# Exponentials row by row on ScalarE for three late score groups of a cross-attention kernel

## The chip, the core and the metric

The kernel runs on one core of one Trainium2 chip. The metric is device time in microseconds (us) of that core; before the change it is 498.44 us, the median of two runs (498.39 and 498.49). The engines are named as in the profile: PE is TensorE (matmuls), PEld its weight loads, DVE is VectorE, ACT is ScalarE, POOL is GpSimd, SP issues most DMAs.

## What is computed

The reference is an image-to-text cross-attention layer with two sets of keys, everything in float32:

```python
# x: (2, 2048, 640), ctx: (2, 154, 1024); 20 heads of 32
q = heads(x @ Wq.T)
text, ip = ctx[:, :77], ctx[:, 77:]
out  = softmax(q @ heads(text @ Wk.T).T / sqrt(32)) @ heads(text @ Wv.T)
out += softmax(q @ heads(ip @ Wk_ip.T).T / sqrt(32)) @ heads(ip @ Wv_ip.T)
return merge(out) @ Wo.T + bo + x
```

So each token and head has two softmaxes over 77 scores each. "A row" below is one such softmax: 77 neighbouring numbers in each of the 128 partitions (tokens).

## The kernel before

Channels lie on the partitions in chunks of 128, which is 4 heads. The work is cut into 20 units u: two images, 5 chunks of channels each, 2 halves of the tokens (1024) each. A unit's 8 tiles of 128 tokens form three groups s: groups 0 and 1 have 3 tiles, group 2 has 2 tiles. With 4 heads and 2 softmaxes per tile, a group of 3 tiles holds 24 rows and a group of 2 tiles holds 16.

The order of all work is written out by hand, in one long list of words (`SCHEDULE`). Each engine then works through its own instructions strictly in that order, and waits where an operand isn't ready or a buffer isn't free. The words for group s of unit u are, in the order in which one group needs them:

- `Rs.u@abcd`: the scores by PE, into four PSUM banks, one for each head (the digits; in the listings bank 0 is bank_79 and bank 7 is bank_86, so bank 1 is bank_80, bank 4 is bank_83, bank 5 is bank_84)
- `Ks.u`: ACT copies the four banks into `pb` in SBUF (line 238)
- `Ms.u`: DVE takes the maximum of each row (line 251)
- `Ss.u`: POOL, sometimes DVE, subtracts the maxima from the scores in place (line 265)
- `Es.u`: ACT takes the exponential, the whole group in one instruction (line 272)
- `Ds.u`, `Is.u`: DVE sums each row (line 297) and inverts the sums (line 304)
- `Ns.u`: POOL multiplies (line 309); `Ts.u`: DVE transposes in place (line 316)

`A.q` then multiplies two units' probabilities with the values on PE (line 325) into four banks, and `CA.q` copies these out on ACT (lines 348 and 352). Between these stand `q.u.h` (PE, a block of queries into one bank, line 194) and `cq.u.h` (ACT scales it into SBUF, line 204), and the products of the output projection: for the first image `m`, `cm`, `o` and `co` with their sums `G`; `p.i@b` (PE, line 464) is the last output chunk of the second image for token block i into bank b. After `A.9`, the last attention, the rest of the second image's projection follows (`F` and `Y`, lines 854 and 802, fed by weight and token sums `V` and `X` on DVE and POOL, lines 834 and 840).

The kernel already has code that takes a group's exponentials row by row, with the negated maximum as the instruction's bias (lines 274 to 284). It is used for a group whose `S` word is missing from the list; every group has one in this kernel.

Of the kernel before, what the change touches and what calls it, by code (L numbers as in the profile page):

```python
# [9 lines left out]
F32 = mybir.dt.float32  # L10
# [5 lines left out]
H, D, TEXT = 20, 32, 77  # L16
# [4 lines left out]
def kernel(  # L21
# [26 lines left out]
    P = 128  # L48
    NC = C // P
    NCC = CC // P  # L50
    G = P // D
# [19 lines left out]
    small = ctx.enter_context(tc.tile_pool(name="small", bufs=4))  # L71
# [141 lines left out]
    def keys_of(u, s):  # L213
        return pb_of(u, s)[:, :, :, : 2 * L]

    def rows_of(u, s):
        return keys_of(u, s).rearrange("p n g (t l) -> p (n g) t l", l=L)
# [26 lines left out]
    def rows_in(ps, n):  # L244
        return ps[:, : n * 2 * L].rearrange("p (n t l) -> p n t l", n=n, t=2)

    def maxima(u, s, ps=None):
        n = GROUPS[s][1] * G
        mx = small.tile([P, n, 2], F32, tag=f"mx{n}", name=f"mx_{u}_{s}")
        if ps is None:  # L250
            nc.vector.tensor_reduce(mx, rows_of(u, s), AX.X, ALU.max, negate=by_rows(u, s))  # L251
        else:
            for g in range(G):
                nc.vector.tensor_reduce(
                    mx.rearrange("p (n g) t -> p g n t", g=G)[:, g],
                    rows_in(ps[g], n // G),
                    AX.X,
                    ALU.max,
                    negate=True,
                )  # L260
        maxs[(u, s)] = mx
# [7 lines left out]
    def exponential(u, s, ps):  # L269
        if not by_rows(u, s):  # L270
            e = keys_of(u, s).rearrange("p n g l -> p (n g) l")
            nc.scalar.activation(e, e, AF.Exp)  # L272
            return
        n = GROUPS[s][1]
        for g in range(G):
            for t in range(n):
                for x in range(2):
                    row = rows_of(u, s)[:, t * G + g, x]
                    nc.scalar.activation(
                        row,  # L280
                        row if copied(u, s) else rows_in(ps[g], n)[:, t, x],
                        AF.Exp,
                        bias=maxs[(u, s)][:, t * G + g, x : x + 1],
                    )

    def copied(u, s):
        return f"K{s}.{u}" in planned

    def by_rows(u, s):
        return f"S{s}.{u}" not in planned  # L290

    dens = {}

# [257 lines left out]
    for t in range(2):  # L551
# [80 lines left out]
    planned = {w.partition("@")[0].removesuffix(".d") for w in SCHEDULE}  # L632
# [6 lines left out]
    def emit(word):  # L639
# [34 lines left out]
        elif k[0] in "KMSEDINT":  # L674
            ps = at[f"R{i}.{x}"]
            if k[0] == "K":
                take(x, i, ps)
            elif k[0] == "M":
                maxima(x, i, None if copied(x, i) else ps)
            elif k[0] == "E":  # L680
                exponential(x, i, ps)
            else:
                more = (eng,) if k[0] in "SN" else ()
                dict(S=subtract, D=sums, I=invert, N=normalise, T=transpose)[k[0]](x, i, *more)
# [94 lines left out]
    for c, stages in enumerate(chains_of):  # L779
        for _, text in stages:  # L780
            for _, t in terms(text):
                for h in range(NH):
                    o = int(t[0]), NH * int(t[1]) + h
# [113 lines left out]
```

## Time and profile before

| | |
|---|---|
| Timed runs | 498.39 and 498.49 us, median 498.44 |
| Span of the profiled execution, first to last instruction | 496.5 us |
| Outside the span (median less span; the profiled execution has no time of its own listed) | 1.9 us |
| PE busy | 489.3 us (99% of the span) |
| DVE busy | 441.2 us (89%) |
| POOL busy | 403.7 us (81%) |
| ACT busy | 241.9 us (49%) |
| Granted TensorE clock, mean | 0.999 |

In the profile's rows a time is counted from the start of the span. PE shows two records for each matmul. "x16" behind a row is the number of instructions merged into it, and the bracket names how long the engine had been idle before it and what released it. A released engine continues in its own order; idle time of an engine that nobody waits for costs nothing.

### The profile page before, as it was taken

What the parts mean: (1) busy time and instruction counts of PE and PEld (TensorE: products, weight loads), DVE (VectorE), ACT (ScalarE), POOL (GpSimd) and SP (SyncE); (2) the same over time, 40 slices, a digit from 0 to 9 for tenths busy, and PEclk for the clock granted to TensorE, in tenths of its full rate; (3) what the DMA queues carried; (4) which work ended last, traced back from release to release, by engine and by line L of the source; (5) the groups of instructions that cost most, each with busy time, mean ns of one, the idle gap of its engine ahead of it and who ended that gap; (6) DMA issues with size and microseconds to landing.
All of it is one profiled execution on the core that took longest, in us unless ns stands there. A gap on an engine that the chain in (4) does not pass through costs nothing.

```text
span 496.5 us, 9743 instructions
## 1 busy us (share of the span) xinstructions
PE 489.3 (99%) x4114; PEld 288.0 (58%) x4114; DVE 441.2 (89%) x404; ACT 241.9 (49%) x423; POOL 403.7 (81%) x173
## 2 busy tenths in 40 slices
PE   8999999999999999999999999999999999999996
PEld 4658548648647556456655655744766575444442
DVE  0078999999989989998999998899899999999886
ACT  1277557757747567567506635545764443100000
POOL 0079959999989999997995899799599999378770
PEclk9999999999999999999999999999999999999999
DMA  8980542511843735715577078345515012510026
GB/s 291 354 213 20 153 107 71 176 51 36 209 133 89 244 108 172 219 16 164 222 243 237 22 241 309 97 150 185 189 65 160 3 45 64 170 62 24 0 106 232
DMA packets 66956, 70.15 MB, mean 141 GB/s; under 512 B 3680, under 2 KB 46688, under 8 KB 66912
## 3 DMA queue, kind: packets, MB, share of 16 engines
q1 hardware_dynamic: 65648, 67.96, 44.0%
q10 hardware_dynamic: 1264, 1.57, 0.9%
q8 instruction: 32, 0.52, 0.4%
q14 instruction: 12, 0.10, 0.1%
HBM read 58.21 MB, written 11.30 MB: 140 GB/s over the span
## 4 chain that ended last, share of the span: by engine, by line
PE 91%; DVE 6%; DMA 1%; ACT 1%; ACTq 0%; issue 0%; DVEq 0%
PE bank L194 35%; PE bank L854 11%; PE bank L325 11%; PE bank L226 10%; PE bank L133 9%; PE bank L483 9%; PE bank L464 4%; PE bank L493 2%; DVE pb L316 2%; DMA x<-in_x_dram 1%; DVE den L297 1%; DVE mx L251 1%; DVE acc L508 0%; DVE acc L512 0%; ACT pb L238 0%
## 5 line engine op out<-in xcount | busy, mean ns | idle before, releaser
L309 POOL TENSOR_TENSOR pb<-pb,rden 128x1848 f32<-128x1848 f32 (+1 forms) x59 | 172.1, 2938 | 24.0 <-DVE rden L304 21.2
L265 POOL TENSOR_TENSOR pb<-pb,mx 128x1848 f32<-128x1848 f32 (+1 forms) x55 | 162.8, 2977 | 35.4 <-DVE mx L251 35.2
L194 PE MATMUL bank<-x,wq 128*128 128x512 f32 x400 | 178.6, 598 | 0.9 <-DMA wq<-in_L_xattn_Wq_dram 0.6
L251 DVE TENSOR_REDUCE mx<-pb 128x24 f32<-128x1848 f32 (+1 forms) x60 | 109.3, 1841 | 31.5 <-ACT pb L238 31.3
L194 PEld LDWEIGHTS bank<-x,wq 128*128 128x128 f32 x400 | 74.0, 190 | 89.3 <-issue 82.0
L238 ACT COPY pb<-bank 128x462 f32<-128x462 f32 (+1 forms) x240 | 102.0, 537 | 44.5 <-PE bank L226 43.9
L272 ACT ACTIVATE pb<-pb 128x1848 f32<-128x1848 f32 (+1 forms) x60 | 94.3, 1584 | 55.0 <-POOL pb L265 54.2
L297 DVE TENSOR_REDUCE den<-pb 128x24 f32<-128x1848 f32 (+1 forms) x60 | 110.0, 1840 | 5.9 <-ACT pb L272 5.7
L316 DVE STREAM_TRANSPOSE pb<-pb 128x1920 f32<-128x1920 f32 (+1 forms) x60 | 113.9, 1923 | 0.9 <-POOL pb L309 0.9
L226 PEld LDWEIGHTS bank<-kT,qT 32*128 32x128 f32 x1280 | 45.9, 184 | 23.6 <-issue 14.2
L226 PE MATMUL bank<-kT,qT 32*128 32x154 f32 x1280 | 56.5, 305 | 1.0 <-ACT pb L238 0.7
L325 PE MATMUL bank<-pb,v 32*32 32x512 f32 x1600 | 55.2, 597 | 0.1
L204 ACT ACTIVATE qT<-bank 128x512 f32<-128x512 f32 x40 | 23.6, 597 | 50.3 <-PE bank L194 50.3
L133 PE MATMUL bank<-wo_ct,aT 128*128 128x154 f32 x320 | 45.5, 296 | 0.0
L133 PEld LDWEIGHTS bank<-wo_ct,aT 128*128 128x128 f32 x320 | 43.0, 188 | 3.6 <-issue 2.7
L325 PEld LDWEIGHTS bank<-pb,v 32*32 32x32 f32 x1600 | 29.5, 103 | 22.9 <-issue 11.7
L464 PE MATMUL bank<-aT,wo_ct 128*128 128x512 f32 x80 | 36.3, 596 | 0.0
L483 PE MATMUL bank<-aT,wo_ct 128*128 128x256 f32 x128 | 32.8, 389 | 0.0
L802 DVE TENSOR_TENSOR x<-x,bank 128x512 f32<-128x512 f32 x36 | 23.6, 684 | 5.2 <-PE bank L854 4.6
L483 PEld LDWEIGHTS bank<-aT,wo_ct 128*128 128x128 f32 x128 | 23.3, 190 | 6.4 <-issue 3.7
L464 PEld LDWEIGHTS bank<-aT,wo_ct 128*128 128x128 f32 x80 | 15.0, 190 | 17.3 <-issue 17.1
L854 PE MATMUL bank<-pb 128*128 128x512 f32 x48 | 22.1, 593 | 0.0
(74 smaller groups left out, 347.6 us busy)
## 6 DMA issues: line engine op xcount, KB each, us to landing
x<-in_x_dram SPq DMA_DIRECT2D x20, 1280.0 KB, 7.7
out_dram<-acc SPq DMA_DIRECT2D x20, 256.0 KB, 2.6
acc<-in_x_dram SPq DMA_DIRECT2D x16, 256.0 KB, 4.0
x<-in_x_dram SPq DMA_DIRECT2D x15, 256.0 KB, 5.7
out_dram<-x SPq DMA_DIRECT2D x15, 256.0 KB, 2.0
v<-scr SPq DMA_DIRECT2D x40, 80.0 KB, 4.1
wq<-in_L_xattn_Wq_dram SPq DMA_DIRECT2D x9, 320.0 KB, 5.3
aT<-in_L_xattn_Wk_dram SPq DMA_DIRECT2D x5, 512.0 KB, 6.9
```

The source lines that it names most:

```text
L133: nc.tensor.matmul(keys_in(out), loaded[n][:, k, :], cT[:, k, :, t, :], start=(k == 0), stop=(k == NCC - 1))
L194: nc.tensor.matmul(pq, wqs[q % 3][:, k, :], xs[place_of(u, h)][:, k, :], start=(k == 0), stop=(k == NC - 1),)
L226: nc.tensor.matmul(ps[g][:, ts(t, 2 * L)], qTs[(u, h)][g * D : (g + 1) * D, ts(st, P)], kT[g * D : (g + 1) * D, c, b].rearrange("p t l -> ...
L238: nc.scalar.copy(keys_of(u, s)[:, :, g], ps[g][:, : n * 2 * L].rearrange("p (n l) -> p n l", n=n))
L251: nc.vector.tensor_reduce(mx, rows_of(u, s), AX.X, ALU.max, negate=by_rows(u, s))
L265: eng.tensor_tensor(rows_of(u, s), rows_of(u, s), maxs[(u, s)].unsqueeze(3).to_broadcast([P, n, 2, L]), ALU.subtract)
L272: nc.scalar.activation(e, e, AF.Exp)
L297: nc.vector.tensor_reduce(dens[(u, s)], rows_of(u, s), AX.X, ALU.add)
L309: eng.tensor_tensor(rows_of(u, s), rows_of(u, s), rdens[(u, s)].unsqueeze(3).to_broadcast([P, n, 2, L]), ALU.mult)
L316: nc.vector.transpose(p, p)
L325: nc.tensor.matmul(pa[r][g * D : (g + 1) * D, :], v4s[q % 2][rows, g, k, :], zones[rows, :, g, k, :], start=(k == 0), stop=(k == NK - 1),)
L483: nc.tensor.matmul(part, w_of[m][:, kp, op], t_of(m, b, i)[:, kp], start=(op == kp == 0 and m in (1, 2, 5)), stop=(op == 1 and kp == 1 and ...
```

## The change

Three groups lose words from the list, and so take other paths:

| Group | Words removed | What is done instead |
|---|---|---|
| 2 of unit 16 (16 rows) | `S2.16` | `K2.16` stays. ACT takes 16 exponentials of 77 from SBUF, each with its own column of maxima as bias |
| 1 of unit 18 (24 rows) | `S1.18`, `D1.18` | `K1.18` stays. ACT takes 24 exponentials with bias; each writes also its row's sum |
| 2 of unit 19 (16 rows) | `K2.19`, `S2.19` | DVE takes the maxima from the four banks (4 instructions instead of 1), and ACT takes 16 exponentials straight from PSUM, with bias |

The maxima of these groups are written negated. The other words stay where they were. The code for the sums is new:

```diff
         n = GROUPS[s][1]
+        if summed(u, s):
+            dens[(u, s)] = small.tile([P, n * G, 2], F32, tag=f"den{n * G}", name=f"den_{u}_{s}")
         for g in range(G):
             for t in range(n):
                 for x in range(2):
...
                         bias=maxs[(u, s)][:, t * G + g, x : x + 1],
+                        accum_out=dens[(u, s)][:, t * G + g, x : x + 1] if summed(u, s) else None,
                     )
...
+    def summed(u, s):
+        return f"D{s}.{u}" not in planned
```

and of the list:

```diff
-        "m1.3@0 cm1.3 G6.3 m3.3 M0.19 G4.3 G7.3.d T1.18 st.3.0 cm3.3 m6.3 cm6.3 R2.19@6734 K2.19 M2.19 S0.19 "
+        "m1.3@0 cm1.3 G6.3 m3.3 M0.19 G4.3 G7.3.d T1.18 st.3.0 cm3.3 m6.3 cm6.3 R2.19@6734 M2.19 S0.19 "
```

On ACT at group 2 of unit 16 there stood, from `E1.16` on to `E2.16`, `cq.18.0` and the first copies of `CA.7`:

```order
L272 ACTIVATE pb<-pb 128x12x154
L272 ACTIVATE pb<-pb 128x8x154
L204 ACTIVATE qT_0_2688<-bank_80 128x512
L352 COPY aT<-bank_84 128x2x4x32 x2
L352 COPY aT<-bank_81 128x2x4x32 x2
```

and now there stands:

```order
L272 ACTIVATE pb<-pb 128x12x154
L281 ACTIVATE pb<-pb,mx_2_2668 128x77 x16
L204 ACTIVATE qT_0_2702<-bank_80 128x512
L358 COPY aT<-bank_84 128x2x4x32 x2
L358 COPY aT<-bank_81 128x2x4x32 x2
```

One instruction became 16 at the same place; what empties bank 1 (bank_80) and the four banks of `A.7` stands behind them.

On ACT at group 1 of unit 18 there stood `E2.18`, `E1.18`, `cq.19.1`, and the copies `CA.8`:

```order
L272 ACTIVATE pb<-pb 128x8x154
L272 ACTIVATE pb<-pb 128x12x154
L204 ACTIVATE qT_1_3108<-bank_84 128x512
L348 COPY aT<-bank_80 128x4x4x32
L348 COPY aT<-bank_82 128x4x4x32
```

and now:

```order
L272 ACTIVATE pb<-pb 128x8x154
L281 ACTIVATE pb,den_1_3035<-pb,mx_1_2928 128x77 x24
L204 ACTIVATE qT_1_3143<-bank_84 128x512
L354 COPY aT<-bank_80 128x4x4x32
L354 COPY aT<-bank_82 128x4x4x32
```

Again the one became many at its place, with `cq.19.1`, which empties bank 5 (bank_84), behind them.

At group 2 of unit 19 ACT had the four copies `K2.19`, then `E0.19` and `E1.19` (x2), `E2.19`, and the first copies of `CA.9`:

```order
L238 COPY pb<-bank_85 128x2x154
L238 COPY pb<-bank_86 128x2x154
L238 COPY pb<-bank_82 128x2x154
L238 COPY pb<-bank_83 128x2x154
L272 ACTIVATE pb<-pb 128x12x154 x2
L272 ACTIVATE pb<-pb 128x8x154
L352 COPY aT<-bank_79 128x2x4x32 x2
```

and now it has:

```order
L272 ACTIVATE pb<-pb 128x12x154 x2
L281 ACTIVATE pb<-bank_85,mx_2_3233 128x77 x4
L281 ACTIVATE pb<-bank_86,mx_2_3233 128x77 x4
L281 ACTIVATE pb<-bank_82,mx_2_3233 128x77 x4
L281 ACTIVATE pb<-bank_83,mx_2_3233 128x77 x4
L358 COPY aT<-bank_79 128x2x4x32 x2
```

The last reader of the four banks moved from ahead of `E0.19` and `E1.19` to behind them, and bank 4 (bank_83) is read last. On PE no row changes its place. Behind these scores stand there, now as before, `p.0` into bank 5, a product `m` into bank 0, and `p.1` into bank 4, here with what each waits for:

```order
L470 MATMUL bank_84<-aT,wo_ct 128x512 x4
L489 MATMUL bank_79<-aT,wo_ct 128x256 [waits DVE_49]
L489 MATMUL bank_79<-aT,wo_ct 128x256 x3
L470 MATMUL bank_83<-aT,wo_ct 128x512 [waits DVE_49,Activation_49]
L470 MATMUL bank_83<-aT,wo_ct 128x512 x3
L489 MATMUL bank_79<-aT,wo_ct 128x256 [waits DVE_49,Pool_49]
```

The fourth row, the first matmul of `p.1`, waited before for ACT alone, which was `K2.19`; now it waits for the maxima on DVE and for the exponentials on ACT.

8 rows, old and new, of the table SCHEDULE are left out of this document.

## The prediction

> **What bounds the kernel now.** I read the page first: the busy times and the chain that ended last. Then the busy time by stretches of the last third, where the change lies.
>
> ```profile
> PE 489.3 (99%) x4114; PEld 288.0 (58%) x4114; DVE 441.2 (89%) x404; ACT 241.9 (49%) x423; POOL 403.7 (81%) x173
> PE 91%; DVE 6%; DMA 1%; ACT 1%; ACTq 0%; issue 0%; DVEq 0%
> ```
>
> ```profile
> 340.00:390.00 50.00, 50.00 (x427) 30.52 (x426) 48.31 (x40) 27.00 (x48) 43.91 (x19) 1.00 0.46 143
> 390.00:426.40 36.40, 36.34 (x319) 22.79 (x317) 36.12 (x38) 14.93 (x22) 34.98 (x19) 1.00 0.18 60
> 433.00:491.99 58.99, 58.99 (x139) 25.89 (x138) 53.88 (x78) 0.94 (x4) 38.63 (x26) 1.00 0.20 76
> ```
>
> The second number of a stretch is its length, the next is PE's busy time. PE has no gap from 340 to 426, where the three groups lie, and none from 433 to the end of its work. Whatever makes PE wait is added to the time in full, because no later gap can take it up. Whatever relieves another engine brings next to nothing. The chain leaves PE for DVE only just before the last attention, and the seam is narrow:
>
> ```profile
> 422.94 3.49 DVE pb L316 x2
> 426.43 0.04 issue
> 426.48 5.13 PE bank L325 x137
> ```
>
> The last transposes release `A.9` at 426.48, and PE had been busy until then. So two engines arrive together there, and taking work from DVE alone moves nothing.
>
> ACT is idle for half of the span, which hides a cost only where nobody waits for what stands behind it in its queue. That is the question for each of the three groups.
>
> **The price of a row.** The trace has no exponential of 77 elements with a bias. The nearest rows, by form and in order of time:
>
> ```profile
> L272 ACT ACTIVATE pb<-pb 128x1848 f32<-128x1848 f32 x40 | 70.0, 1757 | 45.0 <-POOL pb L265 44.2 <-DVE pb L265 0.7
> L272 ACT ACTIVATE pb<-pb 128x1232 f32<-128x1232 f32 x20 | 24.8, 1238 | 9.9 <-POOL pb L265 9.9
> L556 ACT COPY kT<-bank 128x77 f32<-128x77 f32 x4 | 0.7, 226 | 3.3 <-PE bank L133 3.3
> ```
>
> ```profile
> 21.00 0.35 ACT L556 COPY kT<-bank 128x77 f32<-128x77 f32 x2 [1.51 <-PE bank L133]
> ...
> 326.20 1.75 ACT L272 ACTIVATE pb<-pb 128x1848 f32<-128x1848 f32 x1 [1.50 <-POOL pb L265]
> 327.85 0.58 ACT L204 ACTIVATE qT<-bank 128x512 f32<-128x512 f32 x1
> ...
> 408.11 1.38 ACT L238 COPY pb<-bank 128x308 f32<-128x308 f32 x4 [5.09 <-PE bank L226]
> ```
>
> The exponentials' two forms differ by 519 ns for 616 elements, 0.84 ns each; that leaves 0.20 us fixed, and makes 0.265 us for 77 elements standing alone. In a queue instructions overlap: the next one starts 1.65 us after the start of a 1.75 us one, so a step costs 0.10 less, 0.165 us. The cheapest neighbour is the copy of 77 from PSUM: two in 0.35, one of them 0.226, so a step of 0.12. A row's step therefore lies between 0.12 and 0.265 us. I take 0.25, close to the upper row: it is the same operation, and it must fetch a column of maxima, which none of these rows does. From PSUM, the four copies of 308 (1.38 for four, some 0.44 for one) have steps of 0.31, of which 0.26 is elements; their fixed part of 0.05 is 0.04 less than that of the exponentials' step (1.65 less 1.56 of elements, 0.09). So I take 0.21 there, and 0.12 to 0.265 as its bounds. A sum written beside the row is bounded by nothing (a by-product) and by an instruction's whole fixed part, 0.20; I take one fixed step, 0.09, so 0.34 for such a row, with 0.25 and 0.45 as bounds.
>
> [...]
>
> **Group 2 of unit 16.** It removes a subtraction from POOL, and turns one exponential on ACT into 16.
>
> ```profile
> 345.92 1.75 ACT L272 ACTIVATE pb<-pb 128x1848 f32<-128x1848 f32 x1 [2.79 <-POOL pb L265]
> 348.26 1.24 ACT L272 ACTIVATE pb<-pb 128x1232 f32<-128x1232 f32 x1 [0.59 <-POOL pb L265]
> 349.40 0.58 ACT L204 ACTIVATE qT<-bank 128x512 f32<-128x512 f32 x1
> ```
>
> ```profile
> 344.50 3.38 DVE L251 TENSOR_REDUCE mx<-pb 128x16 f32<-128x1232 f32 x2
> ```
>
> ```profile
> 351.11 1.13 PE L483 MATMUL bank<-x 128*128 128x256 f32 x4
> ```
>
> The maxima are the first of the two reductions from 344.50, so they are there before `E1.16` is through. `E2.16` no longer waits for POOL and starts at 345.92 + 1.65 = 347.6. Sixteen rows take 4.0 and end at 351.6. Behind them `cq.18.0` (0.58) ends at 352.15 instead of 349.98. It empties bank 1, and the product `m5.2` on PE wants that bank at 351.11. PE waits **1.0 us**; the old cover was 1.1 us. (At 0.12 a row nothing waits, at 0.265 it is 1.3.) `CA.7` moves by no more than PE does, and what PE feeds is later by the same 1.0.
>
> **Group 1 of unit 18.** It removes a subtraction from POOL and a sum from DVE, and turns one exponential into 24 with sums.
>
> ```profile
> L297 DVE TENSOR_REDUCE den<-pb 128x24 f32<-128x1848 f32 x40 | 82.2, 2058 | 5.9 <-ACT pb L272 5.7
> L251 DVE TENSOR_REDUCE mx<-pb 128x24 f32<-128x1848 f32 x40 | 81.9, 2058 | 5.0 <-ACT pb L238 4.9
> L251 DVE TENSOR_REDUCE mx<-pb 128x16 f32<-128x1232 f32 x20 | 28.1, 1405 | 26.4 <-ACT pb L238 26.4
> ```
>
> The sum was worth 2.06 us of DVE; the maxima's two forms leave a fixed part of 0.1 us an instruction.
>
> ```profile
> 389.62 1.23 ACT L272 ACTIVATE pb<-pb 128x1232 f32<-128x1232 f32 x1 [4.17 <-POOL pb L265]
> 392.87 1.75 ACT L272 ACTIVATE pb<-pb 128x1848 f32<-128x1848 f32 x1 [2.02 <-POOL pb L265]
> 394.52 0.58 ACT L204 ACTIVATE qT<-bank 128x512 f32<-128x512 f32 x1
> ```
>
> ```profile
> 396.27 1.07 PE L226 MATMUL bank<-kT,qT 32*128 32x154 f32 x24
> ```
>
> Its maxima were taken long before. `E2.18` still waits for POOL, 1.0 later than now, at 390.6; the rows follow 1.13 later, at 391.75, and 24 of 0.34 take 8.2, until 399.9. Then `cq.19.1` ends at 400.5. PE's scores `R1.19` need its queries, and bank 5 which it empties; PE gets there at 396.27 + 1.0 = 397.3. It waits **3.2 us** (1.0 if the sum is free, 5.8 at 0.45; the old cover was 1.2 us). DVE's inversion of the sums also waits until 400, but DVE has 2 us less to do and PE is late anyway. PE is now 4.2 late.
>
> **Group 2 of unit 19.** Here the bank is the matter. The four copies freed bank 4 at 409.5; now `E2.19` does, and ACT takes it behind `E0.19` and `E1.19`.
>
> ```profile
> 401.05 1.99 PE L483 MATMUL bank<-aT,wo_ct 128*128 128x256 f32 x8
> ...
> 413.29 3.60 PE L464 MATMUL bank<-aT,wo_ct 128*128 128x512 f32 x8
> ```
>
> ```profile
> 403.61 0.67 DVE L512 TENSOR_TENSOR acc<-acc,bank 128x512 f32<-128x512 f32 x1
> 404.20 2.07 DVE L251 TENSOR_REDUCE mx<-pb 128x24 f32<-128x1848 f32 x1
> ```
>
> ```profile
> 413.29 1.75 ACT L272 ACTIVATE pb<-pb 128x1848 f32<-128x1848 f32 x1 [1.50 <-POOL pb L265]
> 415.50 1.23 ACT L272 ACTIVATE pb<-pb 128x1232 f32<-128x1232 f32 x1 [0.46 <-POOL pb L265]
> ```
>
> `p.1` starts on PE at 413.29, while `E1.19` only starts on ACT. Unmoved, 413.29 + 1.65 + 16 x 0.21 + 0.1 = 418.4 would free the bank: 5.1 us of waiting. PE comes 4.2 later, at 417.5. `E1.19` is later too, by its chain (`R0.19`, `K0.19`, `M0.19`, two subtractions): `M0.19` stands behind `cm1.3` on DVE, which starts 0.6 us behind the end of its product on PE (401.05 + 1.99), so 4.2 - 0.6 = 3.6. Then `E1.19` is at 416.9, the rows from 418.55 to 421.9, and `p.1` goes at 422.0: **4.5 us** of waiting (at 0.265 a row 5.4). Behind `p.1` PE's queue holds `p.2`, `p.3` and `A.9`, all the rest of its work. The four maxima from PSUM cost DVE three more fixed parts (0.1 us each, by the forms above); it has them, since PE is late. `E2.19` ends 5.3 us later than now, and the sums, the multiplication and the transposes ahead of `A.9` follow by as much, within PE's 8.7.
>
> The waits add up to 1.0 + 3.2 + 4.5 = **8.7 us**.
>
> **The clock.** Of the waits of PE that the profile lists, the longest once the work runs is this:
>
> ```profile
> PE bank L226 <- ACT pb L238: 0.7, 1, 0.7
> ```
>
> So this trace shows only at its two ends what a wait of 4 us does.
>
> ```profile
> 1.05 3.16 PE L546 MATMUL bank<-pb 128*128 128x128 f32 x14 [1.05 <-DVE pb L544]
> ...
> 18.69 4.38 PE L133 MATMUL bank<-wo_ct,aT 128*128 128x154 f32 x32
> ```
>
> ```profile
> 491.99:495.40 3.41, 0.75 (x2) 0.00 (x0) 0.69 (x1) 0.00 (x0) 0.00 (x0) 1.00 0.63 233
> 495.40:496.50 1.10, 0.00 (x0) 0.00 (x0) 0.00 (x0) 0.00 (x0) 0.00 (x0) 0.50 0.00 0
> ```
>
> At the start 14 records of 128 columns took 3.16, steps of 0.21, while later 154 columns took 0.13: half speed for the first 3 us. At the end, 0.75 us of matmuls and then 2.65 idle were followed by a granted clock of 0.50. So a wait of 4.5 us probably sends PE back to half speed, and the first 3 us behind it then do 1.5 us of work: **1.5 us** more. At the 3.2 us wait it is less sure, at 1.0 it is excluded.
>
> [...]
>
> **Sum.** The profiled span is 496.5; it becomes 506.7. The 1.9 us between span and median lie outside it and stay: 498.4 + 8.7 + 1.5 = **508.6 us**.
>
> **Rivals.**
>
> *No clock drop*: the three waits alone, 507.1. For it speaks that the only drop seen is at PE's end. Chance 0.2.
>
> *Dearer rows or a second drop*: the 3.2 us wait halves the clock too (+1.5, 510.1), or a sum costs a whole 0.20 (+2.6, 511.2), or both (512.7). Chance 0.25.
>
> *Cheap rows*: at 0.165 without a price for sums, the first two waits vanish (16 rows end at 350.2, 24 at 394.7), and only the bank is left: 413.29 + 1.65 + 16 x 0.12 + 0.1 less 413.29, 3.7, less up to 1 us by which DVE, relieved of 2.0, brings `M0.19` forward to the end of `K0.19`. That is 501.3 to 502.1. It decides where a row is under 0.18. For it speaks the 0.12 of the copies; against it, that they have no operand of their own. With prices in between up to 505. Chance 0.12.
>
> *Not slower*: DVE is the bound, as the chain says of 399 to 426, and the 2.0 us sum taken from it brings `A.9` forward, less 0.3 for the four maxima: 496.7. It decides only if PE has slack ahead of `A.9` that exceeds the bank wait, at least 3 us. PE's 36.34 busy of 36.40 speaks against it. Chance 0.03.
>
> **How the numbers follow.** The forecast itself, waits and one drop, has 0.4. Two per cent, 10 us, is about what a measurement of this kernel can tell from no change; it lies at 508.4, nearly on the forecast. Slower by over 2%: the dearer cases (0.25) and some two thirds of the forecast's: 0.53. Within 2%: 0.45. Faster by over 2% has only mechanisms that I don't see: 0.02. The range of 8 in 10 runs from 503.5 (sums free, no drop and rows a little under 0.25) to 512.5 (sums at 0.45 and two drops).
>
> **What would show it.** In the profile after: ACT line 281 with steps of 0.25, 0.34 and 0.21; PE waiting for ACT line 204 near 351 (1.0) and near 397 (3.2), and for ACT line 281 near 417 (4.5); a granted clock under 1.00 in the stretch behind the last wait. It is wrong if a row's step is outside 0.2 to 0.3, if the sum costs nothing or twice my step, or if the clock stays at 1.00.

## The result, and the profile after

The changed kernel takes 511.06 us (two runs, 510.60 and 511.52) against 498.44: a ratio of 1.0253, 95% interval 1.0236 to 1.0271. The profiled execution is that of 511.52 us and spans 509.7, 13.2 more than before. The page, busy times and the clock by fortieths of the span:

```profile
PE 494.7 (97%) x4114; PEld 290.5 (57%) x4114; DVE 438.1 (86%) x406; ACT 251.5 (49%) x496; POOL 395.8 (78%) x170
...
PEclk9999999999999999999999999999999897999999
```

PE runs the same 4114 records and is busy for 5.4 us longer: the records themselves became longer, and two digits of the clock are below 9. Then the longest waits of PE, as engine and line, what it waited for, and us in total, times, longest:

```profile
PE bank L470 <- ACT pb L281: 4.6, 1, 4.6
PE bank L226 <- ACT qT L204: 3.0, 1, 3.0
PE bank L552 <- DVE pb L550: 1.1, 1, 1.1
PE bank L489 <- ACT qT L204: 1.0, 1, 1.0
PE bank L226 <- ACT pb L238: 0.7, 1, 0.7
```

Three are new: for the query copy behind unit 16's rows (line 489, 1.0), for the one behind unit 18's rows (line 226, 3.0), and of `p.1` for the last rows of unit 19 (line 470, 4.6). The other two, 1.1 and 0.7, were there before. The rows on ACT that cause the new ones, by line:

```profile
L281 ACT ACTIVATE pb<-pb,mx 128x77 f32<-128x77 f32 x40 | 12.3, 344 | 0.0
L281 ACT ACTIVATION_READ_ACCUMULATOR pb<-pb,mx 128x1 f32 x24 | 4.5, 186 | 0.0
L281 ACT ACTIVATE pb<-bank,mx 128x77 f32<-128x77 f32 x16 | 3.5, 372 | 0.0
```

and in order of time:

```profile
347.55 4.09 ACT L281 ACTIVATE pb<-pb,mx 128x77 f32<-128x77 f32 x16
351.55 0.57 ACT L204 ACTIVATE qT<-bank 128x512 f32<-128x512 f32 x1
...
392.04 0.34 ACT L281 ACTIVATE pb<-pb,mx 128x77 f32<-128x77 f32 x1
392.29 0.19 ACT L281 ACTIVATION_READ_ACCUMULATOR pb<-pb,mx 128x1 f32 x1
392.39 0.34 ACT L281 ACTIVATE pb<-pb,mx 128x77 f32<-128x77 f32 x1
...
400.26 0.57 ACT L204 ACTIVATE qT<-bank 128x512 f32<-128x512 f32 x1
...
420.67 3.53 ACT L281 ACTIVATE pb<-bank,mx 128x77 f32<-128x77 f32 x16
```

Sixteen rows of 0.34 within 4.09 make steps of 0.25. Each sum is an instruction of its own, which starts 0.25 behind its row; the next row starts 0.34 to 0.35 behind the last. From PSUM, 3.53 for sixteen of 0.37 makes steps of 0.21.

PE by stretches around and behind the two long waits; the last three columns are the granted clock, the DMA share and the rate in GB/s:

```profile
398.40:401.81 3.41, 0.92 (x18) 0.82 (x18) 1.43 (x3) 3.41 (x16) 2.06 (x4) 1.00 0.00 0
401.82:405.22 3.40, 3.40 (x9) 2.71 (x9) 1.10 (x1) 2.68 (x6) 3.33 (x2) 0.50 0.00 0
405.24:408.60 3.36, 3.36 (x35) 2.66 (x35) 2.14 (x3) 1.22 (x3) 0.00 (x0) 1.00 0.01 2
```

```profile
418.88:422.28 3.40, 0.81 (x4) 0.38 (x2) 3.40 (x6) 3.26 (x9) 1.29 (x3) 1.00 0.43 112
422.30:425.70 3.40, 1.44 (x2) 0.83 (x3) 3.37 (x3) 1.90 (x9) 3.40 (x2) 0.50 0.16 45
425.71:429.11 3.40, 3.40 (x5) 1.33 (x4) 2.30 (x3) 0.00 (x0) 3.40 (x2) 0.50 0.01 2
429.13:432.50 3.37, 3.37 (x14) 2.43 (x13) 0.00 (x0) 0.00 (x0) 2.38 (x4) 1.00 0.00 0
```

Both waits were followed by a clock of 0.50, for 3.4 us behind the first and 6.8 us around the end of the second. `p.1`, 3.60 us before, takes 6.10 (the wait that its row shows is the 4.6 of the list):

```profile
424.26 6.10 PE L470 MATMUL bank<-aT,wo_ct 128*128 128x512 f32 x8 [4.56 <-ACT pb L281]
430.19 1.03 PE L489 MATMUL bank<-aT,wo_ct 128*128 128x256 f32 x4
```

How late PE is at each point shows from the starts of the same matmuls. After the change the scores `R1.19`, `R0.19` and the product `p.3` behind `p.1` start here:

```profile
397.33 0.54 PE L226 MATMUL bank<-kT,qT 32*128 32x154 f32 x6
406.29 1.07 PE L226 MATMUL bank<-kT,qT 32*128 32x154 f32 x24
432.78 7.03 PE L470 MATMUL bank<-aT,wo_ct 128*128 128x512 f32 x16
```

Before, the last two of them started here (`R1.19` at 396.27, `p.1` at 413.29):

```profile
400.05 1.07 PE L226 MATMUL bank<-kT,qT 32*128 32x154 f32 x24
419.31 7.03 PE L464 MATMUL bank<-aT,wo_ct 128*128 128x512 f32 x16
```

So PE is 1.1 us late ahead of unit 18's wait, 6.2 behind that wait and its slow stretch, 11.0 when `p.1` starts, and 13.5 behind the second slow stretch.

### The profile page after: what moved, and what is told of

It reads as the page before. It is cut to its first block, busy times and chain, and to the rows that moved or that the text cites. A ratio compares the mean times of both kernels' runs of the same rounds, so it can differ in the third digit from the quotient of the medians.

```text
span 509.7 us, 9815 instructions
## 1 busy us (share of the span) xinstructions
PE 494.7 (97%) x4114; PEld 290.5 (57%) x4114; DVE 438.1 (86%) x406; ACT 251.5 (49%) x496; POOL 395.8 (78%) x170
## 4 chain that ended last, share of the span: by engine, by line
PE 81%; POOL 8%; ACT 4%; DMA 3%; issue 1%; DVE 1%; SPq 0%; POOLq 0%
PE bank L194 31%; PE bank L860 11%; PE bank L133 9%; PE bank L331 8%; PE bank L226 8%; PE bank L470 6%; PE bank L489 6%; POOL pb L265 4%; POOL pb L315 3%; ACT pb L281 2%; DMA scr<-vS 2%; PE bank L499 2%; DVE mx L251 1%; DMA wq<-in_L_xattn_Wq_dram 1%; ACT pb L238 1%
## 5 line engine op out<-in xcount | busy, mean ns | idle before, releaser
L265 POOL TENSOR_TENSOR pb<-pb,mx 128x1848 f32<-128x1848 f32 (+1 forms) x52 | 155.1, 2999 | 34.8 <-DVE mx L251 34.6
L251 DVE TENSOR_REDUCE mx<-pb 128x24 f32<-128x1848 f32 (+1 forms) x59 | 107.9, 1848 | 31.5 <-ACT pb L238 31.4
L238 ACT COPY pb<-bank 128x462 f32<-128x462 f32 (+1 forms) x236 | 100.6, 541 | 40.9 <-PE bank L226 40.3
L272 ACT ACTIVATE pb<-pb 128x1848 f32<-128x1848 f32 (+1 forms) x57 | 90.1, 1593 | 57.9 <-POOL pb L265 57.1
L303 DVE TENSOR_REDUCE den<-pb 128x24 f32<-128x1848 f32 (+1 forms) x59 | 107.9, 1836 | 7.1 <-ACT pb L272 5.7
L470 PE MATMUL bank<-aT,wo_ct 128*128 128x512 f32 x80 | 38.8, 630 | 4.6 <-ACT pb L281 4.6
L358 ACT COPY aT<-bank 128x256 f32<-128x256 f32 x40 | 11.5, 405 | 25.2 <-PE bank L331 25.0
```

The costliest lines, as they stand in the source:

```text
L238: nc.scalar.copy(keys_of(u, s)[:, :, g], ps[g][:, : n * 2 * L].rearrange("p (n l) -> p n l", n=n))
L265: eng.tensor_tensor(rows_of(u, s), rows_of(u, s), maxs[(u, s)].unsqueeze(3).to_broadcast([P, n, 2, L]), ALU.subtract)
L303: nc.vector.tensor_reduce(dens[(u, s)], rows_of(u, s), AX.X, ALU.add)
```

## The experiments

All ratios are to the kernel before, run beside each kernel (medians 498.22 to 498.36).

**Each group alone.** The words of the other two groups are put back.

```diff
 # back in the first and the second kernel (unit 16 alone, unit 18 alone)
-R2.19@6734 M2.19 ... D0.19 p.0@5
+R2.19@6734 K2.19 M2.19 ... D0.19 S2.19 p.0@5
 # back in the first and the third (unit 16 alone, unit 19 alone)
-cq.19.0 D0.18 ... E1.18 I1.18
+cq.19.0 S1.18 D0.18 ... E1.18 D1.18 I1.18
 # back in the second and the third
-K2.16 M2.16 cq.17.1
+K2.16 M2.16 S2.16 cq.17.1
```

> Only the group of unit 16 has its exponentials row by row; units 18 and 19 are as before. Theory (waits add up): the rows hold up the query copy behind them, PE waits 1.0 us near 351, the granted clock stays at 1.00, and the time is 498.4 + 1.0 = 499.5 us. Rival (the parts only hurt together): this group alone has its row cost hidden by the 1.1 us of cover, 498.4 us.

Measured: 499.82 us, ratio 1.0030 (1.0020 to 1.0040). PE waits where it was said, and no execution's mean clock is under 0.998:

```profile
352.19 1.13 PE L489 MATMUL bank<-x 128*128 128x256 f32 x4 [1.01 <-ACT qT L204]
```

The group costs 1.5 us, its wait and some 0.5 more. In the profiled execution `A.9` also waits 0.3 us for DVE's transposes, which it didn't before; the rest lies within the interval.

> Only the group of unit 18 has its exponentials and sums row by row. Theory (wait and clock): the rows end near 399.0, PE waits 3.3 us for the query copy, near 396 to 399.6; if the clock halves behind it, 1.6 more: 501.7 without and 503.4 us with a drop, and executions may differ by it. Rival (the clock figure costs nothing, the wait is all): 501.7 us in every execution.

Measured: 503.00 us, ratio 1.0089 (1.0064 to 1.0114). PE's wait is 2.8 us by its idle time. The four executions agree far less than the kernel's usually do, and the fastest and the slowest are those with the highest and the lowest mean granted clock: 501.10 us at 1.000, 502.73 at 0.995, 503.26 at 0.997, 504.11 at 0.992. The one with a clock of 1.000 has about the time of the wait alone (498.32 and 2.8; 501.7 was expected for it). The profiled one is the longest; its stretches from the wait on:

```profile
395.28:398.68 3.40, 1.31 (x32) 0.30 (x6) 0.02 (x1) 3.40 (x22) 3.09 (x3) 1.00 0.02 5
398.70:402.09 3.39, 2.71 (x20) 2.31 (x21) 2.53 (x3) 3.39 (x10) 2.60 (x3) 0.50 0.00 0
402.11:405.50 3.39, 3.39 (x9) 2.67 (x9) 0.00 (x0) 0.88 (x3) 1.53 (x1) 0.50 0.00 0
405.52:408.90 3.38, 3.38 (x35) 2.67 (x35) 2.63 (x3) 1.71 (x4) 0.00 (x0) 1.00 0.01 2
```

Here the same wait was followed by two stretches at 0.50, in which PE was busy for 6.1 us. At half speed that is 3.0 us lost, the difference between the longest execution and the shortest.

> Only the group of unit 19 is read from PSUM, row by row. Theory (wait and clock): bank 4 is free at 418.4 instead of 409.5, PE waits 5.1 us from 413.3, and half speed behind it costs 1.7 to 2.4 more: 505.2 to 505.9 us. Rival (the wait is all): 503.5 us. Rival (the reads from PSUM themselves slow ACT or PE): rows dearer than 0.21 us a step.

Measured: 505.70 us, ratio 1.0150 (1.0130 to 1.0169), executions from 504.86 (clock 0.997) to 506.98 (0.992). The wait of `p.1` is the forecast one:

```profile
418.47 5.23 PE L470 MATMUL bank<-aT,wo_ct 128*128 128x512 f32 x8 [5.06 <-ACT pb L281]
```

Its 16 rows take 3.55 us, steps of 0.21, so the rival of dear reads from PSUM falls. The wait alone would be 503.5, and 2.2 are left for the clock. Here the whole of the wait but its end lay ahead of the slow stretch, and one such stretch was all:

```profile
418.18:421.57 3.39, 3.10 (x4) 1.52 (x5) 3.32 (x5) 0.24 (x2) 3.32 (x2) 0.50 0.03 7
421.59:424.90 3.31, 3.31 (x12) 1.97 (x11) 0.66 (x1) 0.00 (x0) 3.31 (x3) 1.00 0.00 0
```

**The same waits with PE kept at work.** Matmuls whose result nobody reads fill the long waits; the waits end when their cause ends.

```diff
-R1.19@4275
+(3 matmuls of 512 columns into bank 4) R1.19@4275
-p.1@4
+(5 matmuls of 512 columns into bank 2) p.1@4
```

> The changed kernel, with matmuls whose result nobody reads put on PE ahead of the two long waits: 3 of 512 columns (2.6 us) into bank 4 ahead of the scores of unit 19's group 1, and 5 (4.3 us) into bank 2 ahead of p.1. The waits end when they did before. Theory (the clock drop costs 4 us of the change): clock 1.00 throughout, 511.1 - 1.6 - 2.4 = 507.0 us. Rival (the waits are all, half speed is only a figure): 511 us as before.

Measured: 507.81 us, ratio 1.0190 (1.0173 to 1.0207), executions from 507.29 to 508.14, clock 0.999 to 1.000. With more work on PE the kernel is 3.2 us faster than the changed one. The added matmuls (line 653), `p.1`, and a stretch behind it:

```profile
418.04 4.45 PE L653 MATMUL bank<-aT,wo_ct 128*128 128x512 f32 x10
422.76 3.70 PE L470 MATMUL bank<-aT,wo_ct 128*128 128x512 f32 x8 [0.27 <-ACT pb L281]
...
424.30:430.00 5.70, 5.70 (x21) 3.65 (x20) 3.17 (x5) 0.00 (x0) 5.62 (x5) 1.00 0.01 1
```

`p.1` still starts when its bank comes free, and takes 3.70 instead of 6.10. So half speed is real time and no mere figure. Of the change's 12.6 us, 9.5 remain without it (507.81 less 498.32). The last group alone, with the five matmuls ahead of `p.1`:

> Only unit 19's group is read from PSUM row by row, with 5 matmuls of 512 columns (4.3 us) into bank 2, which nobody reads, ahead of p.1. The wait for bank 4 ends when it did. Theory (5.1 us of wait, the rest of this group's loss is the clock): 498.4 + 5.1 = 503.5 us in every execution, clock 1.00. Rival (something else of the group costs the 2.3 us above its wait): 505.7 us.

Measured: 503.01 us, ratio 1.0100 (1.0084 to 1.0116), all four executions within 0.7 us, clock 0.999 to 1.000. Without the added matmuls it was 505.70 (clock 0.992 to 0.997); the 2.7 us between them are the clock's.

**The sums.**

```diff
-E1.18 I1.18
+E1.18 D1.18 I1.18     # 24 rows with bias, no accumulator
```

> The changed kernel with the sums of unit 18's group 1 taken by DVE again: its 24 exponentials keep their bias and lose the accumulator. Theory (a second instruction for each sum, 0.09 us of step, makes that wait long): steps of 0.25, the wait near 397 falls from 3.0 to about 1.0 us and leaves the clock at 1.00 there; left are 1.0 + 1.0 + 4.6 and 1.7 to 2.4 for the clock behind p.1: 506.6 to 507.3 us. Rival (it is the number of rows, not the sums): 510 us or more.

Measured: 507.78 us, ratio 1.0188 (1.0174 to 1.0202), 3.3 us less than with sums. On ACT and PE:

```profile
391.92 6.09 ACT L281 ACTIVATE pb<-pb,mx 128x77 f32<-128x77 f32 x24
397.92 0.57 ACT L204 ACTIVATE qT<-bank 128x512 f32<-128x512 f32 x1
```

```profile
PE bank L470 <- ACT pb L281: 4.6, 1, 4.6
PE bank L552 <- DVE pb L550: 1.1, 1, 1.1
PE bank L489 <- ACT qT L204: 1.0, 1, 1.0
PE bank L226 <- ACT qT L204: 0.8, 1, 0.8
```

The wait falls from 3.0 to 0.8, and the half speed behind it is gone (the clock is 1.00 from 394 to 406). The time is 0.5 above the expected range: around `p.1` half speed lasted 6.8 us in the profiled execution (418.77 to 425.57), and its mean clock of 0.993 is that of three executions in four.

**The bank.**

```diff
-R2.19@6734
+R2.19@6732
```

> The changed kernel with one bank exchanged: unit 19's group 2 has its scores in banks 6, 7, 3 and 2 instead of 6, 7, 3 and 4, so that p.1 has bank 4 to itself. The rows on ACT are the same. Theory (the wait is for the bank alone): p.1 starts at once, the 4.6 us and the half speed behind them go; left are 1.0 + 3.3 and up to 2 for the clock behind the scores of unit 19: 502.6 to 504.3 us. Rival (late exponentials hold up the last attention in any case): PE waits as long ahead of A.9, 510 us.

Measured: 505.69 us, ratio 1.0148 (1.0134 to 1.0162). On PE, around `p.1`:

```profile
414.94 3.70 PE L470 MATMUL bank<-aT,wo_ct 128*128 128x512 f32 x8
418.47 1.89 PE L489 MATMUL bank<-aT,wo_ct 128*128 128x256 f32 x8
420.20 3.60 PE L470 MATMUL bank<-aT,wo_ct 128*128 128x512 f32 x8
```

`p.1` follows without a gap while the rows of unit 19 are only to come (421.33 on ACT), and `A.9` starts without a wait: the bank alone was the cause. The total missed its range by 1.4 us. Its waits are 3.0 and 1.0, and its clock is 0.992 in all four executions. In the profiled one half speed lasted 6.8 us (399.13 to 405.94), with PE busy for 5.3 us of it, so some 2.7 us were lost; the top of the range had room for 1.6. The clock fell when PE had waited for only 1.5 of the 3.0 us.

**What stood behind the rows, moved.**

```diff
-E2.16 D2.16 S0.16.d q.18.0@1 cq.18.0
+q.18.0@1 cq.18.0 E2.16 D2.16 S0.16.d
-R2.18@7613 E1.17 D1.17 ... N2.18 E1.18 I1.18
+R2.18@7613 E1.17 E1.18 D1.17 ... N2.18 I1.18
-R2.19@6734
+R2.19@6732
```

> All three groups stay row by row, and what stood behind them is moved: q.18.0 and cq.18.0 ahead of the rows of unit 16, the rows of unit 18 to right behind E1.17 (ACT is idle there for 6.7 us), and the bank exchange of unit 19. Theory (waits alone made the loss): 498.3 to 498.8 us, clock 1.00. Rival (the rows cost something by themselves, in ACT's time or in traffic): over 500 us. Against the kernel before there is nothing to win, since PE has no gap: below 497.8 both are wrong.

Measured: 499.39 us, ratio 1.0024 (1.0014 to 1.0034), clock 0.999 to 1.000. That is 0.6 above the expected range and 0.6 below the rival's 500. The change's three waits are gone from PE's list; one of 1.0 stands there that the change alone didn't have.

> As the kernel with everything moved, but unit 16 is as before the change (its maxima subtracted by POOL, one exponential). Theory: no wait is left at all, 498.3 us as before. Rival (work taken from DVE and POOL shortens the way to the last attention): below 497.8 us.

Measured: 498.80 us, ratio 1.0010 (1.0002 to 1.0019). That is 0.5 more than expected, and not the rival's gain. A wait of 0.5 is left; the next kernel has it too.

> Only unit 18's group is row by row, with its sums, and placed right behind E1.17 where ACT was idle; DVE is rid of one sum (2.06 us), POOL of one subtraction. Theory (PE sets the pace, and DVE's chain to the last attention begins behind PE's products near 400): 498.4 us, no change. Rival (DVE's chain gains the 2.06 us): below 497.8 us.

Measured: 498.74 us, ratio 1.0009 (1.0000 to 1.0019). All 24 rows with their sums and no loss that matters; but no gain either, though DVE had 2 us less to do. In its trace DVE and PE wait at another place:

```profile
386.91 1.44 DVE L251 TENSOR_REDUCE mx<-pb 128x16 f32<-128x1232 f32 x1 [0.86 <-ACT pb L238]
388.26 3.56 DVE L322 STREAM_TRANSPOSE pb<-pb 128x1280 f32<-128x1280 f32 x2
```

```profile
391.92 5.61 PE L331 MATMUL bank<-pb,v 32*32 32x512 f32 x160 [0.45 <-issue]
```

The 8.2 us of rows stand in a gap of ACT that was 6.7 us long before, and now hold up `E0.18` and the score copies `K2.18` behind them. The maxima wait 0.86 for these, the transposes for the maxima, and `A.8` comes half a microsecond late. The wait shrank and moved; no version beats the kernel before.

With unit 19's group row by row as well that wait is 0.5 too, and with unit 16's also 1.0; this agrees with the 0.6 us between those two kernels (498.80 and 499.39). The trace with all three shows the way: unit 16's sums on DVE (line 303, 351.92) wait 1.71 for its rows, the inversion behind them is late, POOL's next multiplication starts at 355.70 instead of 354.15, POOL then works without a gap until 380, and DVE's transposes at 380.25 wait 1.33 for it.

## Why the prediction was right

The forecast was 508.6 us in 503.5 to 512.5, with 0.53 for slower by over 2%; 511.06 lies in the range and over that bound. The chain of causes was right: rows hold up a copy or a bank, PE waits, and half speed follows. One of its terms, the clock, was much too small. The 2% that it takes for about what a measurement of this kernel can tell is too wide: the intervals here reach 0.1 to 0.3% to each side.

**The price of a row**: 0.25, 0.34 with its sum and 0.21 from PSUM, all three as taken. The sum's 0.09 (a row every 0.34 with it, every 0.25 without) is as large as the one fixed step taken for it, and it is an instruction of its own, 186 ns, that the program's order doesn't show and the trace does. The 0.25 was less well founded. It was a choice between bounds of 0.12 and 0.265, and the upper bound was worked out as the time of a lone row; a lone row takes 0.344, of which 0.09 overlaps the next. So the size came out, and the working for it did not; what makes the row longer than 0.265 no run here separates.

**The waits**: 1.0, 3.2 and 4.5 forecast; 1.0, 3.0 and 4.6 measured by PE's idle time. By the starts of the same matmuls they are a little longer. PE is 1.1 us late behind the first. From there to `R0.19` it loses 5.2, of which 3.4 us at half speed explain 1.7, so 3.5 are left for the second wait. From there to `p.1` it loses 4.7. That makes 9.3 us against my 8.7, and the kernel with PE kept at work comes near it with 9.5. That each wait ends where I put it was shown group by group, and for the last by the exchange of the bank.

**The clock** is the term that was mis-sized. I charged one drop of 3 us at half speed, 1.5 us. The changed kernel has two drops, 3.4 and 6.8 us long, that cost about 1.7 us (half of 3.4) and 2.5 us (13.5 less 11.0), 4.2 in all. That is 2.7 of the 3.0 us by which the profiled execution's 13.2 exceeds the forecast's 10.2. The waits bring 0.6 more, and some 0.2 are made up ahead of `A.9`. "Less sure at the 3.2 us wait" was too low: the clock fell there in the profiled execution, and the mean clock was under 1.000 in three executions of four with that group alone. And a drop need not be over after 3 us: half speed lasted 6.8 us in four profiled executions. In the first half of these PE was idle for 2.0 us (the changed kernel at 422.30), 0.7 (unit 18 alone) and 1.5 (bank exchanged); without the sums it was still waiting there at 420. Where PE was idle for only 0.3 us of the first 3.4 (unit 19 alone), that was all. One of the forecast's supports was also weaker than it says: it reads half speed from the slow steps in the first 3 us of the kernel before, but the granted clock listed there is 1.00 (0.00 to 3.88), so only the 0.50 at the end, behind 2.65 us without a matmul, showed the clock fall behind an idle PE.

**The rivals.** *No clock drop* (507.1) is refuted by the 0.50 and by the kernels kept at work. *A second drop* (510.1) is what happened, and dearer than it was priced; the range held the result because it had allowed for it. Its neighbour, a sum at a whole 0.20, fell with the step of 0.34, and *Cheap rows* with that of 0.25; the sum for these left out half speed behind its bank wait of 3.7 us, though in the changed kernel the clock fell to 0.50 at waits of 3.0 and 4.6 us. *Not slower*: DVE's 2 us brought nothing even where the waits behind the rows were nearly gone, 498.74 against 498.22. In that kernel the chain that ended last runs on PE alone from 395 to `A.9` at 427.5, so PE set the time there and DVE had nothing to shorten.

## What to carry to other kernels

An engine that idles for half of the time still delays the bound engine when its work gets longer, by what is queued behind it: look up the next copies that free a bank and the cover they have (1.1 and 1.2 us here), and who reads a bank last. Where PE bounds a kernel, ask of a long wait what the clock does as well: at the waits of 2.8 to 5.1 us here half speed cost 1.6 to 3.0 us more, and nothing in one execution of four with unit 18's group alone; at the changed kernel's wait of 1.0 us the clock stayed at 1.00. Try the order before giving up the change: a copy moved ahead of its rows, rows moved into a gap and a bank exchanged took away all but 1.0 of the 12.6 us, though they won nothing against the kernel before.

## What the runs showed of the hardware that was not expected

Half speed lasted 3.4 us at two places of the profiled executions (401.82 of the changed kernel, 418.18 with unit 19 alone) and 6.8 us at four (422.30 of the changed kernel, unit 18 alone, without the sums, and with the bank exchanged). In the 3.4 us ahead of a fall PE had been busy for 0.81 of 3.40 us and 0.92 of 3.41 (the changed kernel), 1.31 of 3.40 (unit 18 alone), 1.9 of 3.40 (bank exchanged, 395.71 to 399.11) and not at all (unit 19 alone, 414.76 to 418.16): in four of these five it had worked for part of the time. The clock did not fall behind 2.89 of 3.41 (394.98 to 398.39 of the changed kernel). It rose again behind stretches at half speed in which PE had worked for 3.40 of 3.40 us (twice in the changed kernel), 3.39 of 3.39 (unit 18 alone) and 3.10 of 3.39 (unit 19 alone), and not behind 1.44 of 3.40 (the changed kernel) or 2.71 of 3.39 (unit 18 alone). Whether the share of busy time decides or the length of the gap was not told apart, and where a bound lies was not shown.

The sum of a row written by ACT is a second instruction of 186 ns, of which 0.09 us counts in the queue (a row every 0.34 us instead of 0.25): for 24 rows 2.2 us, about what the one reduction on DVE took (2.06).
